# Two heads in each 32 rows: the query and key products of a first attention, packed and spread over its steps

## The chip, the cores and the metric

The kernel runs on one core of a Trainium2 chip. A core has five engines that take their instructions in order, each from its own queue, and that wait for each other through semaphores: TensorE (PE in the profile, with its weight loads shown apart as PEld), VectorE (DVE), ScalarE (ACT), GpSimd (POOL) and SyncE (SP, which here only starts transfers). The metric is the device time of one execution in microseconds (us), lower is better. Before the change three runs took 1332.35, 1331.23 and 1332.3 us, a median of 1332.3.

## What is computed

Two layers, each a cross-attention and a feed-forward, on `x` of 8 images with 256 tokens of 256 numbers, and a context of 8 x 256 tokens of 192 numbers. All is float32. The change touches the first cross-attention only. It has 16 heads of 16 numbers:

```python
q = (x @ Wq).reshape(B, N, 16, 16).transpose(0, 2, 1, 3)        # x is normed first
k = (context @ Wk).reshape(B, M, 16, 16).transpose(0, 2, 1, 3)
v = (context @ Wv).reshape(B, M, 16, 16).transpose(0, 2, 1, 3)
scores = jnp.einsum('bhid,bhjd->bhij', q, k) * 16 ** -0.5
scores = jnp.where(context_mask[:, None, None, :], scores, max_neg)
attn = jax.nn.softmax(scores, axis=-1)
out = jnp.einsum('bhij,bhjd->bhid', attn, v).transpose(0, 2, 1, 3).reshape(B, N, 256) @ Wo
```

After it come a mixture of 8 experts over all tokens, a second cross-attention with 16 heads of 64 numbers, and a channel mix. They are the larger part of the time and stay as they are.

## The kernel before

Tokens and heads. An image `b` has 256 tokens; a pair `p` of images (2p, 2p+1) shares one key tile `KT` of 128 partitions x 4 x 512. The 16 heads stand in four tiles `t` = 0..3 of four heads, each head in its own 32 partitions: rows 0 to 15 hold the 16 numbers of a head, row 16 the mask (for keys) or a one (for queries), row 17 of the keys a one, and row 17 of the queries the negated maximum of the scores. The host pads the weights with zeros to 32 columns for a head, so that a projection writes such a tile of 128 rows in one product. `QT` (128 x 4 x 256) holds an image's queries in the same layout, and has three buffers; `KT` has two.

The functions, by name:
- `keys0(p, t2)` makes two of the four key tiles of a pair: two products of 128 x 512 over the first 128 context numbers, and, from the closure `halves` that runs one step later, two products over the last 64 numbers, the one on the upper and the other on the lower 64 partitions. VectorE then adds `krows` (mask row and ones row) while it copies each tile out of PSUM.
- `queries0(b, t2)` makes two of the four query tiles: four products of 128 x 256, and one ScalarE activation of 128 x 512 that scales and puts the one into row 16 with a bias `cq` (loaded from the host).
- `key_rows(p)` computes `krows` for the pair's tokens from the mask: a reduction and three small VectorE operations, and two operations of 128 x 256 (VectorE for the first pair, GpSimd after that).
- `tokens0(b)` turns an image's normed tokens (made by `normed0`, on GpSimd from image 2 on) with four transposes; `values0(b)` makes the values; `project(b, qb)` is the output projection.
- `scores(q, k)`, `pair_maxima` and `values` are the attention itself. A step `h` makes the scores of one half tile twice: for query rows (`q`), whose maximum VectorE takes into `NM`, and, six steps later, for key rows (`k`), of which ScalarE takes the exponential into `ex`. Both write the same two buffers of PSUM (the tag `big`, two buffers); the two readers take turns on each buffer, and the next step's scores wait for both.

The order. `for h in range(8 * B + 12)` issues the steps. Within a step stand: the scores, the turning back of an output, the second halves of `keys0` and `values0` of the step before, `pair_maxima` (every fourth step), then what the table `whole` lists for this step (entered by `at(h, f)`), and `values` (every fourth step). TensorE, VectorE and GpSimd keep this order, so the `at` calls decide what stands in front of what. Eight steps are one image. In the steady part, an image's `queries0` stand 3 and 1 steps ahead of it, in whole halves of the head tiles, and a pair's `keys0` in steps 4 and 12 of 16. From step 47 on the first group's expert routing is mixed into the steps too.

The profile's line numbers: L103 is a helper through which VectorE and GpSimd operations of these steps go, L74 the matmul helper, L77 the transpose helper, L520 the query activation, L585 the exponential, L502 the copy of turned tokens.

Of the kernel before, what the change touches and what calls it, by code (L numbers as in the profile page):

```python
# [15 lines left out]
P = 128  # L16
# [6 lines left out]
BIG = float(2.0**100)  # L23
EPS = 1e-5


# [37 lines left out]
def kernel(ctx: ExitStack, tc: tile.TileContext, a: dict, out: bass.AP):  # L64
# [219 lines left out]
    with ExitStack() as l0:  # L284
# [3 lines left out]
        def load_ctx(p):  # L288
            cols = slice(512 * p, 512 * (p + 1))
            nc.sync.dma_start(ctx0T[:, cols], a["ctxT"][0:P, cols])  # L290
            if p == 0:
                load_mask(nc.sync, slice(0, 512))

            for h in range(2):
                nc.sync.dma_start(ctx1T[64 * h : 64 * h + 64, cols], a["ctxT"][P:C, cols])
            if p == 0:
                nc.sync.dma_start(cq, a["cq"])

# [4 lines left out]
        maskb = w0.tile([P, B * S], U8, name="maskb")  # L303
        cq = w0.tile([P, 1], F32, name="cq")

# [53 lines left out]

        krows = w0.tile([P, B * S], F32, name="krows")  # L360
        kscale = stat.tile([P, B], F32, tag="kscale", bufs=1, name="kscale")
        kshift = stat.tile([P, B], F32, tag="kshift", bufs=1, name="kshift")
        qscale = stat.tile([P, B], F32, tag="qscale", bufs=1, name="qscale")
        ones = stat.tile([P, 1], F32, tag="kones", bufs=1, name="kones")
        nc.vector.tensor_reduce(ones, ident[:, HD0 + 1 : P : 32], AX.X, ALU.add)

        def key_rows(p):
            two, tok = slice(2 * p, 2 * p + 2), slice(512 * p, 512 * (p + 1))

            tc.keep_in_program_order(  # L370
                vec.tensor_reduce(
                    anyk[:, two], maskb[:, tok].rearrange("p (b k) -> p b k", b=2), AX.X, ALU.max
                )
            )
            vec.tensor_scalar(kscale[:, two], anyk[:, two], cq, BIG, ALU.mult, ALU.mult)
            vec.tensor_scalar(kshift[:, two], kscale[:, two], -1.0, ones, ALU.mult, ALU.add)
            vec.tensor_scalar(qscale[:, two], anyk[:, two], HD0**-0.5, None, ALU.mult)
            for b in (2 * p, 2 * p + 1):
                (gps if p else vec).tensor_scalar(
                    krows[:, S * b : S * (b + 1)],  # L380
                    maskb[:, S * b : S * (b + 1)],
                    kscale[:, b : b + 1],
                    kshift[:, b : b + 1],
                    ALU.mult,
                    ALU.add,
                )

        ssq = stat.tile([P, E], F32, tag="ssq", bufs=1, name="ssq")
# [41 lines left out]

        NMs = [w0.tile([P, 2, 4, P], F32, name=f"NM0_{i}") for i in range(2)]
        for m in NMs:
# [3 lines left out]

        def keys0(p, t2):

            if t2 == 0:
                KT = p0.tile([P, 4, 512], F32, tag="KT", bufs=2, name=f"KT0_{p}")  # L440
                tos[2 * p]["KT"] = tos[2 * p + 1]["KT"] = KT
            KT = tos[2 * p]["KT"]
            tok = slice(512 * p, 512 * (p + 1))
            pk = [ps_mm(f"k0_{p}_{t2}_{h}") for h in range(2)]
            cols = [slice((2 * t2 + h) * P, (2 * t2 + h + 1) * P) for h in range(2)]
            for h in range(2):
                matmul(
                    pk[h], lhsT=wk[:, 0, cols[h]], rhs=ctx0T[:, tok], start=True, stop=False
                )

            def halves():
                for h in range(2):
                    r = slice(64 * h, 64 * h + 64)
                    matmul(
                        pk[h], lhsT=wk[r, 1, cols[h]], rhs=ctx1T[r, tok], start=False, stop=True
                    )
                for h in range(2):
                    tc.keep_in_program_order(
                        vec.tensor_tensor(
                            KT[:, 2 * t2 + h, :], pk[h], krows[:, tok], ALU.add  # L460
                        )
                    )

            return halves
# [38 lines left out]

        def queries0(b, t2):
            if t2 == 0:
                tos[b]["QT"] = p0.tile([P, 4, S], F32, tag="QT", bufs=3, name=f"QT0_{b}")
            pq = ps_mm(f"q0_{b}_{t2}").rearrange("p (t n) -> p t n", t=2)
            for i in range(2):
                t = 2 * t2 + i
                for c in range(2):  # L510
                    matmul(
                        pq[:, i, :],
                        lhsT=wq[:, c, t * P : (t + 1) * P],
                        rhs=tos[b]["xT"][:, c, :],
                        start=(c == 0),
                        stop=(c == 1),
                    )

            ways = 1 if (b, t2) == (0, 0) else 2
            nc.scalar.activation(  # L520
                tos[b]["QT"][:, 2 * t2 : 2 * t2 + ways, :],
                pq[:, 0:ways, :],
                AF.Identity,
                bias=cq,
                scale=qscale[:, b : b + 1],
            )
            if ways == 1:
                vec.tensor_scalar(
                    tos[b]["QT"][:, 1, :],
                    pq[:, 1, :],  # L530
                    qscale[:, b : b + 1],
                    cq,
                    ALU.mult,
                    ALU.add,
                )

        def scores(q, k):
# [8 lines left out]
            if k:  # L546
                b, t, kc = k
                for j in range(4):
                    r = slice(32 * j, 32 * j + HD0 + 2)
                    matmul(  # L550
                        sc[j // 2][:, j % 2, 1, :],
                        lhsT=tos[b]["KT"][r, t, b % 2 * S + kc * P : b % 2 * S + (kc + 1) * P],
                        rhs=tos[b]["QT"][r, t, :],
                        start=True,
                        stop=True,
                    )
            if q:
                b, t, qb = q
                for j in range(4):
                    r = slice(32 * j, 32 * j + HD0 + 1)  # L560
                    matmul(
# [10 lines left out]
            for i in range(2):  # L572
                if q:
                    vec.tensor_reduce(
                        NMs[(2 * b + t // 2) % 2][
                            :, qb, t, HD0 + 1 + 64 * i : 64 * i + 64 : 32
                        ],
# [12 lines left out]
        def pair_maxima(b, t2, to):  # L590
# [3 lines left out]
            for i in range(2):  # L594
                for qb in range(2):
                    transpose(pt[:, i, qb * P : (qb + 1) * P], nm[:, qb, 2 * t2 + i, :])
            qt = to["QT"][:, 2 * t2 : 2 * t2 + 2, :]
# [68 lines left out]

        tos += [{} for b in range(B)]
        stats0 = [ln_tiles(0, 2, "l0_0")]
        second = keys0(0, 0)
        tokens0(0)  # L670
        key_rows(0)
        second()
        queries0(0, 0)
        stats0 += [ln_tiles(2, 2, "l0_1")]
# [5 lines left out]
        for b, h in ((2, 4), (3, 6), (4, 15), (5, 23), (6, 31), (7, 39)):  # L680
            at(h, lambda b=b: normed0(b))
        at(0, lambda: keys0(0, 1))
        at(1, lambda: queries0(0, 1))
        at(1, lambda: tokens0(1))
        at(2, lambda: values0(0))
        at(3, lambda: queries0(1, 0))
        at(3, lambda: key_rows(1))
        at(4, lambda: keys0(1, 0))
        at(5, lambda: queries0(1, 1))
        at(6, lambda: tokens0(2))  # L690
        at(6, lambda: values0(1))
        at(7, lambda: queries0(2, 0))
        at(8, lambda: tokens0(3))
        at(9, lambda: queries0(2, 1))
        at(11, lambda: keys0(1, 1))
        for p in range(1, 4):
            h, b = 16 * (p - 1), 2 * p
            if h:
                at(h, lambda b=b: tokens0(b))
                at(h + 3, lambda p=p: key_rows(p))  # L700
                at(h + 4, lambda p=p: keys0(p, 0))
                at(h + 5, lambda b=b: queries0(b, 0))
                at(h + 7, lambda b=b: queries0(b, 1))
                at(h + 8, lambda b=b: tokens0(b + 1))
                at(h + 12, lambda p=p: keys0(p, 1))
            at(h + 13, lambda b=b: queries0(b + 1, 0))
            at(h + 15, lambda b=b: queries0(b + 1, 1))
            at(h + 17, lambda b=b: values0(b))
            at(h + 25, lambda b=b: values0(b + 1))

# [12 lines left out]
        for b in range(B):  # L723
            for qb in range(2):
                at(8 * b + 19, lambda b=b, qb=qb: project(b, qb, tos[b]))

# [3 lines left out]
        lgs = [[v.rearrange("p e d -> p (e d)") for v in u] for u in lgs]  # L730
        ems = [krows[:, 0:1024], krows[:, 1024:2048], wk.rearrange("p c f -> p (c f)")]
        dt = wq
# [973 lines left out]
```

## Time and profile before

| | us |
|---|---|
| median of three runs | 1332.3 |
| the profiled execution, its span | 1332.8 |
| first score product of the first attention (step 0) | 11.69 |
| step 9 begins | 41.48 |
| step 24 begins | 87.73 |
| step 40 begins (16 steps: 50.50) | 138.23 |
| step 47 begins | 160.92 |
| TensorE busy, whole span | 1315.3 (99%) |
| VectorE busy, whole span | 567.7 (43%) |
| ScalarE busy, whole span | 576.6 (43%) |
| GpSimd busy, whole span | 245.1 (18%) |

A row of the profile's list of groups gives the line, the engine, the operation, what it writes and reads, the shapes, the count, the busy time and the mean of one in ns, and then the idle time of the engine ahead of these instructions with what ended it. A line of the timeline gives start, length, engine, line, operation and count; the bracket at its end is the idle time of the engine ahead of it. TensorE runs a float32 product as two instructions, so that a 128 x 256 product counts twice. A line of the table of stretches gives the stretch and its length, then for PE, PEld, DVE, ACT and POOL the busy time with the number of instructions, the granted clock of TensorE (1.00 is full), the DMA share and GB/s.

### The profile page before, as it was taken

The page shows a single profiled execution, that of the slowest core. Times are in us where ns is not written, and L with a number is a line of the kernel's source. Part 1 is how long each engine was busy: PE and PEld are TensorE (multiplying, and loading weights), DVE is VectorE, ACT ScalarE, POOL GpSimd, SP SyncE. Part 2 cuts the span into 40 slices and gives each one's busy share as a digit, 9 for nine tenths or more (in the row PEclk, how much of TensorE's full clock was granted, in tenths as well). Part 3 has the DMA queues.
Part 4 walks back from the last instruction along what each step waited for, and adds up shares of the span by engine and source line. Part 5 has one row for each costly group of instructions (what it writes and reads, how often), then busy time and mean ns, then how long its engine had stood idle before and what let it go on. Part 6 is the DMA issues. An engine that isn't in the chain of part 4 may idle for free.

```text
span 1332.8 us, 19111 instructions
## 1 busy us (share of the span) xinstructions
PE 1315.3 (99%) x7520; PEld 955.6 (72%) x7520; DVE 567.7 (43%) x1131; ACT 576.6 (43%) x1396; POOL 245.1 (18%) x285
## 2 busy tenths in 40 slices
PE   9999999999999999999999999999999999999998
PEld 5666655577778786788867888866676676677777
DVE  6677777433320233322333110024544544544675
ACT  2644455353522363423634122213545445445653
POOL 3222412200000010100101000012323323333423
PEclk9999999899999999999999999999999999999999
DMA  7100000134134232342323434350000000000001
GB/s 218 65 1 2 1 1 1 63 103 134 68 134 134 70 132 78 124 134 72 130 82 120 134 118 151 103 154 1 0 1 1 1 1 1 1 1 1 1 8 56
DMA packets 59145, 86.85 MB, mean 65 GB/s; under 512 B 3376, under 2 KB 49072, under 8 KB 59056
## 3 DMA queue, kind: packets, MB, share of 16 engines
q1 hardware_dynamic: 58480, 85.11, 19.5%
q8 instruction: 59, 0.97, 0.3%
q10 hardware_dynamic: 576, 0.52, 0.1%
q14 instruction: 30, 0.25, 0.1%
HBM read 83.53 MB, written 2.10 MB: 64 GB/s over the span
## 4 chain that ended last, share of the span: by engine, by line
PE 94%; ACT 4%; DVE 2%; issue 0%; POOL 0%; ACTq 0%; DVEq 0%; POOLq 0%
PE ph L1104 17%; PE pe L1120 16%; PE sc L74 9%; PE q L74 7%; PE o L74 7%; PE po L74 5%; PE k L74 5%; PE pe L77 4%; PE v L74 4%; PE pc L1146 4%; PE pf L1050 3%; PE ln L968 3%; PE pf L74 1%; PE pk L74 1%; PE pr L74 1%; PE ln L74 1%
## 5 line engine op out<-in xcount | busy, mean ns | idle before, releaser
L1112 ACT ACTIVATE ht<-ph,b 128x256 f32<-128x256 f32 x256 | 119.3, 474 | 371.6 <-PE ph L1104 371.2
L1104 PE MATMUL ph<-slots,w 128*128 128x256 f32 x1024 | 266.9, 384 | 0.9 <-ACT ht L1112 0.2
L1120 PE MATMUL pe<-w,ht 128*128 128x256 f32 x1024 | 263.3, 381 | 0.0
L1104 PEld LDWEIGHTS ph<-slots,w 128*128 128x128 f32 x1024 | 182.3, 189 | 54.0 <-ACT ht L1112 21.7
L1120 PEld LDWEIGHTS pe<-w,ht 128*128 128x128 f32 x1024 | 192.0, 190 | 29.9 <-DVE slots L1129 4.2
L1379 POOL TENSOR_TENSOR ex<-ex,rz 128x1024 f32<-128x1024 f32 x64 | 119.9, 1895 | 229.9 <-DVE rz L1377 222.4
L1366 ACT ACTIVATE ex<-sc,nm 128x256 f32<-128x256 f32 x256 | 117.4, 484 | 53.0 <-DVE nm L1361 53.0
L585 ACT ACTIVATE ex<-sc 128x512 f32<-128x512 f32 x128 | 75.1, 598 | 68.7 <-PE sc L74 64.9
L74 PE MATMUL sc<-KT,QT 17*128 17x256 f32 (+1 forms) x1024 | 103.5, 380 | 0.8 <-ACT QT L520 0.7
L1028 POOL TENSOR_TENSOR es<-es,zs 128x1024 f32<-128x1024 f32 x12 | 22.7, 1894 | 432.8 <-DVE zs L1027 432.8
L103 DVE TENSOR_REDUCE NM<-sc 128x2 f32<-128x512 f32 x128 | 87.6, 691 | 32.7 <-PE sc L74 27.6
L1129 DVE TENSOR_TENSOR slots<-pe,b 128x512 f32<-128x512 f32 x32 | 22.1, 692 | 185.1 <-PE pe L1120 185.1
L74 PE MATMUL q<-xT,wq 128*128 128x256 f32 x384 | 94.9, 391 | 0.9 <-DVE xT L1276 0.9
L74 PEld LDWEIGHTS sc<-KT,QT 17*128 17x128 f32 (+1 forms) x1024 | 75.9, 186 | 20.8 <-issue 11.6
L74 PEld LDWEIGHTS q<-xT,wq 128*128 128x128 f32 x384 | 69.2, 189 | 28.1 <-issue 14.4
L1361 DVE TENSOR_REDUCE nm<-sc 128x4 f32<-128x1024 f32 x64 | 75.4, 1219 | 7.7 <-PE sc L74 4.7
L74 PE MATMUL po<-wo,ot 128*128 128x256 f32 x320 | 72.5, 382 | 0.0
L77 PE MATMUL pe<-ident,ex 128*128 128x128 f32 x512 | 70.2, 278 | 0.8 <-DVE et L1395 0.7
L74 PEld LDWEIGHTS po<-wo,ot 128*128 128x128 f32 x320 | 60.1, 190 | 10.9 <-issue 3.2
L77 PEld LDWEIGHTS pe<-ident,ex 128*128 128x128 f32 x512 | 56.5, 140 | 15.3 <-issue 7.6
L1395 ACT COPY et<-pe 128x512 f32<-128x512 f32 x64 | 37.5, 599 | 63.9 <-PE pe L77 63.4
L74 PE MATMUL o<-et,V 128*64 128x256 f32 x512 | 62.8, 385 | 0.8 <-ACT ot L1414 0.8
(227 smaller groups left out, 1665.9 us busy)
## 6 DMA issues: line engine op xcount, KB each, us to landing
w<-in_w_dram SPq DMA_DIRECT2D x64, 1024.0 KB, 5.7
b<-in_b_dram SPq DMA_DIRECT2D x32, 128.0 KB, 6.8
x_sb<-in_x_dram SPq DMA_DIRECT2D x3, 512.0 KB, 7.0
ctx0T<-in_ctxT_dram SPq DMA_DIRECT2D x4, 256.0 KB, 8.6
ctx1T<-in_ctxT_dram SPq DMA_DIRECT2D x8, 128.0 KB, 8.0
se<-in_slots_dram SPq DMA_DIRECT2D x1, 1024.0 KB, 11.1
wq<-in_wq_dram SPq DMA_DIRECT2D x1, 1024.0 KB, 5.1
wo<-in_wo_dram SPq DMA_DIRECT2D x1, 1024.0 KB, 12.1
```

The source lines that it names most:

```text
L74: tc.keep_in_program_order(nc.tensor.matmul(out, lhsT=lhsT, rhs=rhs, start=start, stop=stop))
L77: tc.keep_in_program_order(nc.tensor.transpose(out, in_, ident))
L103: ins = op(*args, **kwargs)
L585: nc.scalar.activation(ex[:, 2 - 2 * i : 4 - 2 * i, :], sc[1 - i][:, :, 1, :], AF.Exp)
L968: nc.tensor.matmul(pl[:, m * 512 : (m + 1) * 512], lhsT=st["xnT"][:, c, t * P : (t + 1) * P], rhs=snT[:, c, m * 512 : (m + 1) * 512], star ...
L1104: nc.tensor.matmul(ph, lhsT=c_["w1"][:, c, hc * P : (hc + 1) * P], rhs=slots[e][:, c * 256 : (c + 1) * 256], start=(c == 0), stop=(c == 1),)
L1112: nc.scalar.activation(ht, ph, AF.Gelu, bias=b1[:, e, hc : hc + 1])
L1120: nc.tensor.matmul(c_["pe"][:, b, :], lhsT=c_["ht"][hc][:, b * SL : (b + 1) * SL], rhs=c_["w2"][:, hc, :], start=(hc == 0), stop=(hc == HI ...
L1146: nc.tensor.matmul(pc[:, :D], lhsT=CT[:, bl, e, t * P : (t + 1) * P], rhs=eos[e][:, bl, :], start=(e == 0), stop=(e == E - 1),)
L1361: nc.vector.tensor_reduce(nm, sc, AX.X, ALU.max, negate=True)
L1366: nc.scalar.activation(ex[:, i, qb, :], sc[:, i, qb, :], AF.Exp, bias=nm[:, i, qb : qb + 1], accum_out=z[:, i, qb : qb + 1],)
L1379: nc.gpsimd.tensor_tensor(ex, ex, rz.rearrange("p h q -> p (h q)").unsqueeze(2).to_broadcast([P, 4, S]), ALU.mult,)
```

## The change

Each 32 rows now hold two heads in the projections' products: rows 0 to 15 one, rows 16 to 31 the other. `pack` makes the packed weights `wkd` and `wqd` on the core, with GpSimd copies out of the padded weights. A product then gives two of the four tiles at once (`u` = 0, 1 in place of `t` = 0..3), and two copies out of PSUM make the tiles `2u` and `2u + 1` from it: each multiplies by a factor for each row (`held`) that is 1 for its own 16 rows and 0 for the other 16. The mask and maximum rows of the odd tiles stand below their head (rows 15 and 14), and their score products read all 32 rows. `key_rows` makes two sets of `krows`, one for each of the two kinds of tile.

The order changes with it: a pair's keys are made in one place (step 7 of 16, the second half in step 8), with one of the two products in the PSUM buffer of the attention's output (`ps_o`); the queries of images 1 and 2 in one piece, of later images in two (4 and 5 steps into the eight for even images, 5 and 7 for odd ones); `tokens0(2)` moves from step 6 to step 5; the second half of the output projection of images 1, 3 and 5 moves one step later. The load of `cq` is gone, and `NM` is half as large.

```diff
-            vec.tensor_scalar(kscale[:, two], anyk[:, two], cq, BIG, ALU.mult, ALU.mult)
-            vec.tensor_scalar(kshift[:, two], kscale[:, two], -1.0, ones, ALU.mult, ALU.add)
-            vec.tensor_scalar(qscale[:, two], anyk[:, two], HD0**-0.5, None, ALU.mult)
-            for b in (2 * p, 2 * p + 1):
-                (gps if p else vec).tensor_scalar(
...
+            for v in range(2):
+                vec.tensor_scalar(
+                    kscale[:, v, two], anyk[:, two], masked[v], BIG, ALU.mult, ALU.mult
+                )
+                vec.tensor_scalar(
+                    kshift[:, v, two], kscale[:, v, two], -1.0, ones[v], ALU.mult, ALU.add
+                )
+                vec.tensor_scalar(
+                    qscale[:, v, two], anyk[:, two], held[v], HD0**-0.5, ALU.mult, ALU.mult
+                )
+                for b in (2 * p, 2 * p + 1):
+                    (gps if p or v else vec).tensor_scalar(
+                        krows[:, p % 2, v, S * (b % 2) : S * (b % 2 + 1)],
...
+        def pack(to, w, u):
+
+            for c in range(2):
+                gps.tensor_copy(
+                    to[:, u, c, :].rearrange("p (j s e) -> p j s e", j=4, s=2),
+                    w[:, c, :].rearrange("p (u s j e) -> p u j s e", u=2, s=2, j=4)[
+                        :, u, :, :, 0:HD0
+                    ],
+                )
+
+        def keys0(p, us):
...
+            pk = [(ps_o if u and len(us) > 1 else ps_mm)(f"k0_{p}_{u}") for u in us]
+            for i, u in enumerate(us):
                 matmul(
-                    pk[h], lhsT=wk[:, 0, cols[h]], rhs=ctx0T[:, tok], start=True, stop=False
+                    pk[i], lhsT=wkd[:, u, 0, :], rhs=ctx0T[:, tok], start=True, stop=False
                 )
...
+                for i, u in enumerate(us):
+                    for v in range(2):
+                        tc.keep_in_program_order(
+                            vec.scalar_tensor_tensor(
+                                KT[:, 2 * u + v, :],
+                                pk[i],
+                                held[v],
+                                krows[:, p % 2, v, :],
+                                ALU.mult,
+                                ALU.add,
+                            )
                         )
...
+            for v in range(2):
+                qt = tos[b]["QT"][:, 2 * us[0] + v : 2 * us[-1] + v + 1 : 2, :]
+                if v and b == 0 and us[0] == 0:
+                    vec.tensor_scalar(
+                        qt, pq, qscale[:, v, b : b + 1], masked[v], ALU.mult, ALU.add
+                    )
+                else:
+                    nc.scalar.activation(
+                        qt, pq, AF.Identity, bias=masked[v], scale=qscale[:, v, b : b + 1]
+                    )
...
+        pack(wkd, wk, 0)
+        pack(wqd, wq, 0)
         stats0 = [ln_tiles(0, 2, "l0_0")]
-        second = keys0(0, 0)
+        second = keys0(0, (0,))
...
-        at(0, lambda: keys0(0, 1))
-        at(1, lambda: queries0(0, 1))
+        at(0, lambda: pack(wkd, wk, 1))
+        at(0, lambda: pack(wqd, wq, 1))
+        at(0, lambda: keys0(0, (1,)))
+        at(1, lambda: queries0(0, (1,)))
...
-        at(3, lambda: queries0(1, 0))
+        at(3, lambda: queries0(1, (0, 1)))
         at(3, lambda: key_rows(1))
-        at(4, lambda: keys0(1, 0))
-        at(5, lambda: queries0(1, 1))
-        at(6, lambda: tokens0(2))
+        at(5, lambda: tokens0(2))
         at(6, lambda: values0(1))
-        at(7, lambda: queries0(2, 0))
+        at(7, lambda: keys0(1, (0, 1)))
         at(8, lambda: tokens0(3))
-        at(9, lambda: queries0(2, 1))
-        at(11, lambda: keys0(1, 1))
...
+        at(9, lambda: queries0(2, (0, 1)))
+        for b in range(3, B):
+            h = 8 * (b - 2)
+            if b > 3:
                 at(h, lambda b=b: tokens0(b))
...
+            if b % 2:
+                at(h + 5, lambda b=b: queries0(b, (0,)))
+                at(h + 7, lambda b=b: queries0(b, (1,)))
+            else:
+                at(h + 4, lambda b=b: queries0(b, (0,)))
+                at(h + 5, lambda b=b: queries0(b, (1,)))
+                at(h + 3, lambda b=b: key_rows(b // 2))
+                at(h + 7, lambda b=b: keys0(b // 2, (0, 1)))
```

## Prediction

> **What bounds the stage.** The page's busy times come first: TensorE 1315.3 of 1332.8 us, so work taken off it should shorten the span. Then I cut the first attention into steps, at each step's first score product in the timeline. Steps 32 and 33:
>
> ```profile
> 112.99 0.71 PE L74 MATMUL sc<-QT,KT 18*128 18x256 f32 x8
> ...
> 114.06 0.66 PE L77 MATMUL nm<-ident,NM 128*128 128x128 f32 x4
> 114.17 1.45 DVE L103 TENSOR_REDUCE NM<-sc 128x2 f32<-128x512 f32 x2 [0.69 <-PE sc L74]
> ...
> 114.29 1.21 ACT L585 ACTIVATE ex<-sc 128x512 f32<-128x512 f32 x2 [0.41 <-PE sc L74]
> ...
> 114.56 0.60 PE L77 MATMUL pt_x<-ident,xh_l 128*128 128x128 f32 x4
> ...
> 115.55 0.82 PE L74 MATMUL sc<-QT,KT 18*128 18x256 f32 x8 [0.39 <-ACT ex L585]
> ```
>
> A step's scores take 1.07 us (112.99 to 114.06). The next scores need the two buffers back, that is the two exponentials and two maxima: 2.56 us (115.55 - 112.99). That is a floor: TensorE had 2.1 us of work and waited 0.39. Steps 32 to 39 last 2.56, 2.68, 3.61, 3.01, 3.38, 4.06, 2.94 and 3.00: only work above 2.56 lengthens a step. VectorE is close behind, as step 20 shows:
>
> ```profile
> 73.87 0.71 PE L74 MATMUL sc<-QT,KT 18*128 18x256 f32 x8
> ...
> 74.29 0.65 DVE L103 TENSOR_REDUCE anyk<-maskb 128x2 f32<-128x512 uint8 x1
> ...
> 75.77 0.68 DVE L103 TENSOR_TENSOR x_sb<-po,x_sb 128x512 f32<-128x512 f32 x1
> 76.37 1.27 DVE L103 TENSOR_REDUCE NM<-sc 128x2 f32<-128x512 f32 x2
> ...
> 77.73 0.31 PEld L74 LDWEIGHTS sc<-QT,KT 18*128 18x128 f32 x8 [0.93 <-ACT ex L585]
> ```
>
> The scores were ready near 75.05, but VectorE still had the key rows and the projection's addition; the maxima came at 76.37, and the step took 3.86 where TensorE's work was about 3.4. The groups of steps 24 to 39, and one of the expert stage:
>
> ```profile
> L103 DVE TENSOR_REDUCE NM<-sc 128x2 f32<-128x512 f32 x32 | 22.1, 693 | 8.2 <-PE sc L74 7.1
> L585 ACT ACTIVATE ex<-sc 128x512 f32<-128x512 f32 x32 | 19.0, 598 | 21.8 <-PE sc L74 21.2 <-DVE NM L103 0.5
> ...
> L103 DVE TENSOR_TENSOR KT<-k,krows 128x512 f32<-128x512 f32 x4 | 2.6, 681 | 0.0
> ...
> L103 POOL TENSOR_SCALAR krows<-maskb,kscale,kshift 128x256 f32<-128x256 uint8 x2 | 1.1, 565 | 2.3 <-DVE qscale L103 2.3
> ...
> L1154 DVE SCALAR_TENSOR_TENSOR x_sb<-pc,rzn,x_sb 128x256 f32<-128x256 f32 x16 | 7.7, 484 | 77.0 <-PE pc L1146 77.0
> ```
>
> **What is taken away.** Four query products take 1.92 us (105.12 to 107.04 in the timeline). Each image needed eight and needs four: 8 x 1.92 = 15.4. Two key products take 1.81 and their second halves 1.06, where the two run beside each other; pairs 1 to 3 lose one such set each (8.6), pair 0 goes from 5.74 to about four single products of 0.91 (2.1). In all 26.1 us of TensorE work.
>
> **What of it the floor leaves.** With the new places, a step lasts the larger of its TensorE work and 2.58 (the floor and a little). Steps 16 to 23: 2.58, 2.58, 3.57 (values), 3.00 (projection), 2.58, 2.58, 2.94, 2.90 (keys), together 22.7; steps 24 to 31: 3.14 (key halves, maxima, turned tokens), 2.58, 3.57, 2.58, 2.58, 2.58, 2.94, 2.58, together 22.6. The 16 steps 24 to 39 give 45.3 against 50.5. Over steps 9 to 46 the same count gives 107.2 against 119.4 (160.92 - 41.48): -12.2. Step 47 goes from 3.44 to 2.58: -0.9. Together -13.1.
>
> **What comes back on VectorE, ScalarE and GpSimd.** The copies do not halve: each of a pair's four key tiles still takes one, and all four now come in one step with a third input. The trace has no such form at 128 x 512 out of PSUM. Bounds: 0.64, the spacing of two of today's additions (1.28 for two), and 0.97, twice the 128 x 256 row above. I take 0.72, near the lower end, as L1154 is only a seventh above an addition of its size (0.42). In step 24 (and 8, 40) VectorE then has the maxima until 2.6, four copies until 5.5 and the addition to QT until 6.1; the maxima of step 25 end their first half at 6.75, an exponential follows, and step 26 can begin at 7.45 where the count above had 3.14 + 2.58 = 5.7: +1.7, three times, 5.1. At 0.64 it is 1.4 each, at 0.97 it is 2.7.
>
> Key rows: three more small VectorE operations, about 0.6 us, in steps 19 and 35, where the cover of 3.4 to 3.9 us in steps 20 and 36 shrinks to 2.5 of TensorE work. By the chain of step 20 shown above that costs 1.9 and 1.2: 3.1. Query copies: `QT` of image 4 takes the buffer of image 1, whose last scores are in step 21. The copies of step 20 must wait for those, and the exponentials of step 21 stand behind them on ScalarE, and step 22's scores behind these: two copies of 0.56 (the one 128 x 256 row of L520), some 1.0 in steps 21 and 37: 2.0. Step 10, with two query copies of 0.78 ahead of its exponentials: 0.4. Sum 10.6; net -2.5.
>
> **The first nine steps.** GpSimd packs two 128 x 128 blocks before the first keys and two before the first queries. Bounds for a block: 0.20 (its 128 x 4 operations) and 0.61 (half of a 128 x 256 at 1.22); I take 0.4. The weights land first anyway, at about 8.3 for the queries, so these products start near 9.15 instead of 9.04; but only two of four stand ahead of the first scores, and the key rows no longer wait for `cq` (VectorE waited 1.1 us for it). The start gains about 0.7, of which the packing could take half. Then GpSimd is late:
>
> ```profile
> 29.79 4.84 POOL L103 TENSOR_SCALAR xh_l<-x_sb,mvp_l,rstdp_l 128x256 f32<-128x256 f32 x4
> ...
> 32.81 0.66 PE L77 MATMUL pt_x<-ident,xh_l 128*128 128x128 f32 x4
> ```
>
> Image 2's normed tokens were done at 32.24 and turned at 32.81, in step 6. Now two more `krows` operations (1.13) stand in front of them, TensorE has lost 4.9 us of keys and queries in steps 4 and 5, and the transposes are moved up to step 5. TensorE gets there near 28.0, the tokens are ready near 32.7: it waits 4.7 us, with all later scores behind it. Step 9 then starts near 43.1 against 41.48: +1.6, start included. So far: -13.1 + 10.6 + 1.6 = -0.9.
>
> **The clock.** Work turned into waits has a price that the sum lacks:
>
> ```profile
> 63.84:67.25 3.41, 2.72 (x25) 1.70 (x23) 2.83 (x6) 2.40 (x5) 0.00 (x0) 1.00 0.02 5
> 237.92:241.33 3.41, 1.82 (x13) 1.11 (x12) 1.94 (x6) 3.41 (x9) 0.00 (x0) 1.00 0.00 0
> 241.33:244.75 3.42, 2.75 (x13) 2.35 (x13) 1.38 (x2) 1.09 (x3) 0.00 (x0) 0.50 0.00 0
> 244.75:248.16 3.41, 3.41 (x28) 1.75 (x32) 0.69 (x1) 1.63 (x8) 0.00 (x0) 0.50 0.01 2
> ```
>
> These are stretches of half the 6.83 us for which the granted clock stood at 0.50 (241.33 to 248.16). It fell after a stretch with TensorE busy for 1.82 of 3.41 us, and held in one with 2.72. In the new order, TensorE waits 4.7 us in step 5, and 1.5 to 2.2 in steps 9, 11, 20, 21, 25, 37 and 41. Step 5 surely halves the clock; the products of steps 6 and 7 at half rate cost about 1.6. Of the seven others, some 2.5 should hit a stretch that holds most of the wait (it depends on where the stretches lie). A drop costs between 0 (the next steps wait anyway) and 3.4 (all of 6.83 us at half rate); a step with 2.04 us of work grows from 2.58 to 4.08, which over 6.83 us is 2.5; I take 2.2. So 1.6 + 2.5 x 2.2 = 7.1.
>
> The Trainium skill ("TensorE: Matmul & The Clock Gate", section "HAM oscillation") has the clock fall after idle gaps of more than some 3.4 us. By that rule only step 5 would trip it, and the sum would be 1333.0. The row above, where a wait of 1.46 us was enough, speaks against it.
>
> **Sum.** -0.9 + 7.1 = +6.2. The profiled execution (1332.8) lies 0.5 above the median, so: 1332.8 + 6.2 - 0.5 = 1338.5.
>
> **The rivals.**
> - The clock holds. For: 2.46 of 3.41 us near 910 did not trip it, and most of the new steps keep TensorE busy for 2.04 of 2.58. Against: the drop at 241.33. Then 1332.3 - 0.9 = 1331.4, or 1333.0 with step 5 alone: no change.
> - The gain stays. Place: the maxima of the steps after the key copies and key rows. If VectorE's chain is shorter than I count, the 10.6 is not given back, and -13.1 + 1.6 gives 1320.8: faster. It decides once four copies and an addition end within about 4.4 us of their step's start (6.1 by my count). Against it stands step 20, which was late already.
> - The clock stays low. If a busy share near 0.6 to 0.75 already trips it, about eight drops of 2.5 us follow: 1332.3 - 0.9 + 20 = 1351.
> - The change does not do what it says: excluded as far as the instruction order shows, since the products are halved there.
>
> **How the numbers follow.** Forecast 0.55, clock holds 0.25, gain stays 0.10, clock stays low 0.10. A measurement here can tell about 0.2%, 2.7 us, from nothing. Faster: the gain that stays (0.10) and the fast edge of the clock that holds (0.04): 0.14. Same: 0.17 of the clock that holds and 0.02 of the forecast: 0.19. Slower: 0.67. The range runs from 1330 (the lower edge of the clock that holds) to 1347 (four or five more drops, or copies of 0.97); it leaves out the gain that stays and most of the clock that stays low. The forecast's own range is 1334 to 1345.
>
> **What would show it.** Right: steps 11 to 13, 27 to 29 and 45 near 2.6; a 4 to 5 us wait of TensorE for GpSimd's `xh_l` near 28; steps 20, 25, 36 and 41 above 3.7 with late maxima; stretches at clock 0.50 between 30 and 160 us. Wrong: full clock all through the attention, key copies at another price, or steps 20 and 25 near 2.6. If the span from the first scores to the experts changes by much less than the total, the cause is elsewhere.

## The result, and the profile after

The changed kernel is slower: 1342.9 us (four runs, 1342.57 to 1344.32) against 1332.3, a ratio of 1.0084 (95% interval 1.0072 to 1.0096), so 10.6 us. The page of the changed kernel, its busy times, TensorE and its granted clock over 40 slices of 33.5 us:

```profile
span 1340.7 us, 18958 instructions
## 1 busy us (share of the span) xinstructions
PE 1306.4 (97%) x7424; PEld 945.6 (71%) x7424; DVE 571.2 (43%) x1148; ACT 578.0 (43%) x1407; POOL 250.3 (19%) x301
...
PE   7899999999999999999999999999999999999998
...
PEclk8789999999999999999999999999999999999999
```

Work did go: 8.9 us less of TensorE's busy time. But the first three digits of the clock fell, and the busy time holds what ran at half rate. Starts of steps, from the timelines:

| starts at (us) | before | changed | changed - before |
|---|---|---|---|
| step 0 | 11.69 | 11.09 | -0.60 |
| step 9 | 41.48 | 48.34 | +6.86 |
| step 24 | 87.73 | 100.45 | +12.72 |
| step 40 | 138.23 | 149.29 | +11.06 |
| step 48 | 164.36 | 173.43 | +9.07 |
| step 69 | 236.55 | 246.19 | +9.64 |
| end of the span | 1332.8 | 1340.7 | +7.9 |

The time is lost before step 24 (12.72 us); from there to step 48 the change gains 3.65 us back, as it was meant to. The table of stretches of the changed kernel (TensorE's busy time is the first pair behind the length, the clock the third number from the end):

```profile
11.68:15.10 3.42, 2.21 (x14) 0.90 (x10) 2.79 (x9) 0.30 (x1) 0.32 (x2) 1.00 0.85 269
15.10:18.51 3.41, 3.41 (x9) 1.39 (x6) 2.06 (x4) 0.00 (x0) 0.00 (x0) 0.50 1.04 332
28.75:32.16 3.41, 1.77 (x12) 0.83 (x11) 3.34 (x11) 0.72 (x2) 2.67 (x12) 1.00 0.48 93
32.16:35.58 3.42, 0.47 (x1) 0.18 (x1) 1.10 (x3) 0.00 (x0) 3.42 (x5) 0.50 1.03 396
49.23:52.64 3.41, 2.18 (x16) 1.44 (x8) 3.38 (x8) 1.38 (x5) 0.00 (x0) 1.00 0.00 0
56.06:59.47 3.41, 2.00 (x33) 1.26 (x26) 2.90 (x9) 1.59 (x4) 0.86 (x3) 1.00 0.00 0
59.47:62.88 3.41, 3.06 (x21) 1.97 (x20) 1.97 (x3) 1.59 (x4) 2.16 (x11) 0.50 0.00 0
86.78:90.19 3.41, 1.29 (x18) 0.72 (x16) 2.86 (x7) 0.84 (x2) 2.91 (x10) 1.00 0.00 0
90.19:93.60 3.41, 3.41 (x20) 2.38 (x20) 1.90 (x4) 2.77 (x6) 1.29 (x7) 0.50 0.00 0
```

Four times the clock halves behind a stretch in which TensorE was busy for 1.29 to 2.21 of 3.41 us: at 15.10, 32.16 and 59.47 for 10.24 us, at 90.19 for 6.83. Other stretches as thin passed, such as that of 2.18 at 49.23. The forecast wait of step 5, in the timeline:

```profile
27.92 0.71 PE L77 MATMUL sc<-KT,QT 17*128 17x256 f32 x8
...
31.27 2.18 POOL L106 TENSOR_SCALAR krows<-maskb,kscale,kshift 128x256 f32<-128x256 uint8 x4
...
33.43 4.83 POOL L106 TENSOR_SCALAR xh_l<-x_sb,mvp_l,rstdp_l 128x256 f32<-128x256 f32 x4
34.71 0.47 PE L80 MATMUL pt_x<-ident,xh_l 128*128 128x128 f32 x1 [3.00 <-POOL xh_l L106]
35.91 0.90 PE L80 MATMUL pt_x<-ident,xh_l 128*128 128x128 f32 x3 [0.73 <-POOL xh_l L106]
```

Four key-row operations of GpSimd stand ahead of the normed tokens, and TensorE waits 3.73 us (3.00 + 0.73) for the tokens. The clock fell at 32.16, when the first of these waits (from 31.71 on) had lasted 0.45 us; the stretch ahead of it, with 1.77 us of work, holds a wait of 1.18 us for the maxima of step 4 as well (up to 30.41). Step 20 has the late maxima:

```profile
84.44 0.71 PE L77 MATMUL sc<-QT,KT 32*128 32x256 f32 x8
...
84.86 0.65 DVE L106 TENSOR_REDUCE anyk<-maskb 128x2 f32<-128x512 uint8 x1
...
87.20 0.68 DVE L106 TENSOR_TENSOR x_sb<-po,x_sb 128x512 f32<-128x512 f32 x1
87.80 1.28 DVE L106 TENSOR_REDUCE NM<-sc 128x2 f32<-128x512 f32 x2
...
89.16 0.71 PE L77 MATMUL sc<-QT,KT 32*128 32x256 f32 x8 [2.12 <-ACT ex L614]
```

The addition comes 2.34 us after the reduction of the mask began (87.20 - 84.86; before 1.48, 75.77 - 74.29), since eight small operations lie between (before five): six of the key rows (before three) and two of the expert slots. The step lasts 4.72 us against 3.86. And in step 24 the four key copies:

```profile
102.99 2.72 DVE L106 SCALAR_TENSOR_TENSOR KT<-k,krow,krows 128x512 f32<-128x512 f32 x4
...
105.63 0.68 DVE L106 TENSOR_TENSOR QT<-nm,QT 128x512 f32<-128x512 f32 x1
106.22 1.28 DVE L106 TENSOR_REDUCE NM<-sc 128x2 f32<-128x512 f32 x2
...
107.59 0.71 PE L77 MATMUL sc<-QT,KT 18*128 18x256 f32 x8 [0.51 <-ACT ex L614]
```

Step 25 begins at 103.61 and ends at 107.59: 3.98 us, where the forecast without the copies was 2.58. The table of stretches for just this step has TensorE busy for 2.84 us of it and VectorE for all of it:

```profile
103.61:107.59 3.98, 2.84 (x25) 1.82 (x24) 3.98 (x8) 1.78 (x3) 0.00 (x0) 1.00 0.00 0
```

### The profile page after: what moved, and what is told of

It reads as the page before. It is cut to its first block, busy times and chain, and to the rows that moved or that the text cites. A ratio compares the mean times of both kernels' runs of the same rounds, so it can differ in the third digit from the quotient of the medians.

```text
span 1340.7 us, 18958 instructions
## 1 busy us (share of the span) xinstructions
PE 1306.4 (97%) x7424; PEld 945.6 (71%) x7424; DVE 571.2 (43%) x1148; ACT 578.0 (43%) x1407; POOL 250.3 (19%) x301
## 4 chain that ended last, share of the span: by engine, by line
PE 90%; ACT 4%; DVE 4%; issue 1%; POOL 1%; DMA 0%; ACTq 0%; DVEq 0%; POOLq 0%
PE ph L1134 17%; PE pe L1150 16%; PE sc L77 9%; PE o L77 7%; PE q L77 5%; PE po L77 5%; PE pe L80 4%; PE v L77 4%; PE pc L1176 4%; PE k L77 4%; PE pf L1080 3%; PE ln L998 3%; ACT ex L614 1%; PE pf L77 1%; PE pk L77 1%; PE pr L77 1%
## 5 line engine op out<-in xcount | busy, mean ns | idle before, releaser
L77 PE MATMUL sc<-KT,QT 64*128 64x256 f32 (+2 forms) x1024 | 107.6, 394 | 3.0 <-DVE NM L106 2.4
L77 PEld LDWEIGHTS sc<-KT,QT 64*128 64x128 f32 (+2 forms) x1024 | 78.4, 194 | 23.6 <-issue 11.8
L77 PE MATMUL q<-xT,wq 128*128 128x256 f32 x256 | 63.0, 391 | 0.9 <-DVE xT L1306 0.9
L77 PE MATMUL sc<-QT,KT 32*128 32x256 f32 (+1 forms) x512 | 49.8, 448 | 10.5 <-ACT ex L614 10.5
```

The source lines that it names most:

```text
L77: tc.keep_in_program_order(nc.tensor.matmul(out, lhsT=lhsT, rhs=rhs, start=start, stop=stop))
```

## The experiments

**The clock by itself.** If the low clock is what the change pays, TensorE must be kept busy without anything else being moved. The fill is transposes of the identity into a spare PSUM buffer, at the end of five steps, and in the same way ahead of the token transposes of step 5:

```diff
+        fills = {0: 6, 9: 7, 11: 8, 20: 12, 36: 6}
...
+            if h in fills:
+                to = ps_o(f"fill_{h}")
+                for i in range(fills[h]):
+                    transpose(to[:, 0:P], ident)
```

> The changed kernel with idle TensorE time filled: transposes of the identity into a spare PSUM buffer at the end of steps 0 (6), 9 (7), 11 (8), 20 (12) and 36 (6), and 18 ahead of the token transposes of step 5, in waits of 1.2 to 3.7 us. Nothing else moves. Theory (the halved clock costs most of the 10.6 us, and a stretch of 3.41 us with TensorE busy for less than some 2.2 us halves it): no stretch at clock 0.50 between 8 and 110 us, the time falls to 1335.5 (1333 to 1338). Rival (the products at half rate fall into steps that wait for VectorE or GpSimd anyway): the clock stays up but the time stays above 1340. Rival (the clock does not follow the busy share): the stretches at 0.50 stay, time 1343 to 1346.

Measured: 1332.59 us, ratio to the kernel before 1.0002 (0.9992 to 1.0011). Pure waste, 57 transposes, makes the changed kernel 10.3 us faster. The fill of step 5 in its timeline, then one stretch at the place of the drop of 59.47 (step 12) and the one with the wait of step 20, behind which the drop of 90.19 had come:

```profile
29.15 2.19 PE L80 MATMUL fill_tokens<-ident 128*128 128x128 f32 x18
...
32.25 0.33 PE L80 MATMUL pt_x<-ident,xh_l 128*128 128x128 f32 x1 [0.91 <-POOL xh_l L106]
33.45 0.55 PE L80 MATMUL pt_x<-ident,xh_l 128*128 128x128 f32 x3 [0.88 <-POOL xh_l L106]
```

```profile
54.72:58.13 3.41, 2.63 (x37) 1.73 (x31) 2.43 (x7) 1.63 (x5) 2.00 (x10) 1.00 0.02 5
78.61:82.02 3.41, 2.60 (x24) 2.22 (x26) 3.34 (x9) 0.71 (x2) 3.08 (x9) 1.00 0.00 0
```

The wait of step 5 is still there (2.19 filled, 0.91 and 0.88 left: 4.0 us), so it is not the wait that was removed. Two short drops of 3.41 us stay (at 20.58 and 34.24), all others are gone. So the first theory holds in its cause, not in its sizes: it had excluded any drop here, and 1332.59 lies just below its range. What is left without low clock is no gain and no loss: step 9 starts at 44.48 (+3.0 against before), step 48 at 163.50 (-0.86). From the start of step 9 to that of step 48 it takes 119.02 us against 122.88, 3.9 less.

**GpSimd's order.** The one edit: `at(3, lambda: key_rows(1))` becomes `at(4, ...)`, which puts the rows behind `normed0(2)`.

> The changed kernel with the key rows of pair 1 made in step 4, behind image 2's normed tokens on GpSimd, in place of step 3, in front of them. Theory (TensorE's wait in step 5 is for GpSimd, whose four key-row operations of 2.18 us stand ahead of the tokens): image 2's tokens are ready 2.2 us after the roots earlier, the wait of step 5 shrinks by 2.2, step 9 starts near 46.2 in place of 48.34, the time is 1340.7; other stretches of low clock may move by one in either way (2.5 us each). Rival (step 5 is late for the clock and the statistics alone): step 9 within 0.5 of 48.3, time 1342 to 1344.

Measured: 1335.45 us, ratio 1.0026 (1.0014 to 1.0038). The forecast part is there: from GpSimd's first operation for these tokens to their first transpose it takes 4.70 us (25.95 to 30.65) against 6.70 (28.01 to 34.71). Step 9 starts at 46.41, close to the 46.2 of the theory, but that is partly luck: the first drop lasted 6.83 us in place of 10.24, the second 13.65 in place of 10.24, and the two nearly cancel. And the time gained 7.4 us and not 2.2: in this execution the third drop did not come (the stretches ahead of it had 2.21 and 2.00 busy) and the fourth lasted 3.41. Ten runs of this one kernel spread from 1331.91 (mean granted clock 0.993) to 1340.09 (0.987), so which drops come, and for how long, differs from execution to execution; a single such comparison can't price an edit here.

**Packing without the new order.** Products and copies as in the change, at the places that keys, queries, tokens and projections had before:

```diff
+        at(3, lambda: queries0(1, (0,)))
+        at(4, lambda: keys0(1, (0,)))
+        at(5, lambda: queries0(1, (1,)))
+        at(6, lambda: tokens0(2))
...
+            at(h + 4, lambda p=p: keys0(p, (0,)))
+            at(h + 12, lambda p=p: keys0(p, (1,)))
```

> The packed products of the changed kernel at the places that keys, queries, tokens and projections had before: two key copies or two query copies in a step, never four. Theory (the gain is given back because four key copies, doubled key rows and moved tokens meet in few steps): the steps of queries and keys end near 2.6 each, about 0.44 us less in each of some 20 query places and 0.5 to 0.9 in six key places, no wait of TensorE above 2 us in step 5 and at most one stretch of low clock: 1325 (1322 to 1329). Rival (the doubled copies and key rows themselves eat the gain, wherever they stand): 1331 or more. Rival (steps of 2.04 us of work in 2.58 are too thin for the clock): several stretches at 0.50 after 40 us, 1335 or more.

Measured: 1335.96 us, ratio 1.0028 (1.0016 to 1.004). The first theory fell with its number. The number and the drops of the last rival are what the trace shows, at 13, 78, 133 and 242 us; its reason, steps too thin for the clock, is not, as a single wait of 1.42, 2.13, 1.23 and 1.46 us stands at each:

```profile
9.91:13.32 3.41, 1.77 (x10) 0.61 (x10) 2.95 (x9) 0.54 (x2) 1.00 (x4) 1.00 0.82 254
...
74.76:78.17 3.41, 1.28 (x8) 0.45 (x10) 3.34 (x11) 0.95 (x2) 2.99 (x8) 1.00 0.00 0
...
129.37:132.79 3.42, 2.27 (x19) 1.16 (x20) 2.69 (x5) 1.56 (x3) 0.73 (x2) 1.00 0.00 0
...
238.60:242.01 3.41, 1.82 (x13) 1.11 (x12) 1.86 (x5) 3.41 (x9) 0.00 (x0) 1.00 0.00 0
```

Between the drops the steps are shorter, as expected (24 to 36: 35.20 us against 37.12 before). Step 20 lasts 4.72 here too, though keys stand in it and not queries: what it shares with the changed kernel is the doubled key rows.

**The two cures, alone and together.** At the old places again: (a) fill; (b) the six small key-row operations of pairs 2 and 3 on GpSimd; (c) both.

```diff
+            small = gps if p > 1 else vec
             for v in range(2):
-                vec.tensor_scalar(
+                small.tensor_scalar(
                     kscale[:, v, two], anyk[:, two], masked[v], BIG, ALU.mult, ALU.mult
```

> Packed products at the old places, with TensorE's waits filled by transposes of the identity at the end of steps 0 (6), 4 (6), 20 (12), 36 (6) and 69 (7). Theory (without low clock the old places keep about 1.1 us in steps 9 to 20, 1.9 in 24 to 36 and 2.3 in 40 to 48 against before, and lose 0.9 and 0.4 in steps 20 and 36; the stretches of low clock of the run without fill, at 13, 78, 133 and 242 us, cost the rest): no stretch at 0.50 after 20 us, 1326 (1324 to 1329). Rival (the fill only helped where the order had changed): 1333 or more. Rival (filling takes TensorE time that the steps need): steps 20 and 36 longer than 4.72 and 3.82, 1331 or more.

> Packed products at the old places, with the six small operations of the key rows of pairs 2 and 3 on GpSimd in place of VectorE, nothing filled. Theory (steps 20 and 36 last 4.72 and 3.82 because VectorE does 1.5 us of small operations ahead of the projection's addition and the maxima): step 20 falls to 3.2 and step 36 to 2.9 (some 2.4 us together), TensorE's wait there shrinks from 2.13 to under 0.7, the stretches of low clock at 78 and 133 us go: 1330 (1328 to 1332.5). Rival (the projection's addition or the slots' scale on VectorE sets these steps): step 20 above 4.0, time 1334 to 1337.

> Both: key rows' small operations of pairs 2 and 3 on GpSimd, and fill at the end of steps 0 (6), 4 (6), 20 (3), 36 (3) and 69 (7). Theory (late VectorE and low clock are what gives the gain back, and they add up): 1324 (1321 to 1327), the fastest of all, no low clock after 20 us. Rival (with the waits gone the steps of 2.58 themselves trip the clock): stretches at 0.50 in places without a long wait, 1329 or more.

Measured: (a) 1325.83 us, ratio 0.9943 (0.9931 to 0.9956); (b) 1327.15, 0.9958 (0.9946 to 0.9971); (c) 1321.58, 0.9917 (0.9904 to 0.9931). (a) is the forecast to 0.2 us, and its steps 20 and 36 keep their 4.71 and 3.81, so the fill takes nothing from them; one early drop stays in its profile (17.36 to 24.18). (b) is faster than its range, and shortens step 20 to 3.23 and step 36 to 2.56, 2.75 us together; its timeline has the addition at once behind the slots' operations, and the rows beside it:

```profile
79.78 0.26 POOL L106 TENSOR_SCALAR kscale<-anyk,krow 128x2 f32<-128x2 f32 x1 [2.30 <-DVE nt_slots L106]
...
79.89 0.68 DVE L106 TENSOR_TENSOR x_sb<-po,x_sb 128x512 f32<-128x512 f32 x1
...
80.49 1.27 DVE L106 TENSOR_REDUCE NM<-sc 128x2 f32<-128x512 f32 x2
...
81.84 0.71 PE L77 MATMUL sc<-QT,KT 32*128 32x256 f32 x8 [0.64 <-ACT ex L615]
```

With the wait of step 20 down from 2.13 to 0.64 us the drops at 78 and 133 are gone too, without fill. The one at 242 is gone as well, though this edit does not touch that place; in the kernel before, too, only some executions have it, as shown further down. Two early ones stay (at 12.19 and 32.67). (c) has the clock at 1.00 until its last microsecond, so steps of 2.58 us do not lower the clock by themselves. It is the fastest of all: 10.5 us faster than before, 21.3 faster than the change as it stands.

**What the new order costs with both cures.** The same cures on the changed kernel's own order, with the key rows of pair 1 one step later (`at(4, ...)`).

> The changed kernel with its own order, but the key rows of pair 1 in step 4, the six small key-row operations of pairs 2 and 3 on GpSimd, and the waits filled (steps 0, 9, 11, 20, 36, 69 with 6, 7, 8, 3, 3, 7 transposes, and 10 ahead of the tokens of step 5). Theory (beside late VectorE and low clock, the new order itself costs: TensorE waits for GpSimd's tokens in step 5, and four key copies delay the maxima in steps 8, 24 and 40): 1327.5 (1325.5 to 1330), some 6 us behind the same cures at the old places; steps 25 and 41 stay near 3.97. Rival (the order is harmless once the clock holds and VectorE is freed): within 2 us of 1321.6.

Measured: 1329.2 us, ratio 0.9972 (0.9962 to 0.9982). The order is not harmless, but the 7.6 us between the medians are not all its own, since the fill does not hold the clock here. The profiled execution starts step 48 at 159.21, that of (c) at 153.36. Of the 5.85 us, 2.95 lie ahead of step 9, where the wait for GpSimd is still 0.73 + 0.88 us behind 1.31 of fill, and where two drops of 3.41 us stay (at 18.61 and 32.26). The other 2.90 come at full clock: 1.06 in steps 9 to 18, 1.34 in steps 24 to 27, where step 25 with its four key copies still takes 3.97 against 2.74, and 0.50 elsewhere. The one run with a mean clock of 0.999 took 1326.09, 4.5 above (c); this is the nearest that the record has to the price of the order alone.

**The drop of the kernel before.** The same fill there, seven transposes at the end of step 69.

> The kernel before with seven transposes of the identity at the end of step 69, in its 1.46 us wait at 239.73. Theory (a wait of 1.46 us, with TensorE busy for 1.82 of 3.41 us, halves the clock for 6.83 us, which costs some 1.8 us): no stretch at 0.50 near 241, 1330.5. Rival (the stretch at half rate lies beside waits for ScalarE): within 0.5 of 1332.2. Rival (the clock falls there for another reason): the stretch stays.

Measured: 1331.98 us, ratio 0.9996 (0.9987 to 1.0005). The drop is gone from the profile:

```profile
237.18:240.59 3.41, 2.93 (x23) 2.22 (x21) 1.96 (x6) 3.41 (x10) 0.00 (x0) 1.00 0.00 0
240.59:244.01 3.42, 2.39 (x24) 1.90 (x28) 1.64 (x5) 2.29 (x8) 0.00 (x0) 1.00 0.01 2
```

and from step 69 to the end the span is 2.85 us shorter (1093.4 against 1096.25). But the median is what it was: the number is the rival's, though a drop was there and had its price. The runs explain it: in each of these experiments a profiled execution's own time lies 1.75 to 2.2 us above its span (here 1331.45 and 1329.7; for (c) 1321.01 and 1318.8). So the profiled execution of before, with a span of 1332.8, took about 1334.8, and belongs to the few: of the 49 times of before in the three sets of comparisons 9 lie at 1334.1 to 1334.9, the others at 1331.1 to 1332.8. The mean granted clock that is recorded with each of them agrees: 0.997 in all nine, which is what one drop of 6.83 us at half clock makes of a span of 1332.8 (1 - 0.5 x 6.83 / 1332.8), and 0.998 to 1.0 in the other 40. In the filled kernel it is 1.0 in all eleven.

**A last wait.** (c) with image 1's token transposes in step 2 in place of step 1.

> The fastest version so far (old places, small key-row operations on GpSimd, fill) with image 1's token transposes in step 2 behind the values' first half, in place of step 1, where TensorE waits 1.29 us for VectorE's normed tokens. Theory (that wait is on the path): steps 1 and 2 together 0.8 to 1.3 us shorter, 1320.6. Rival (the next scores wait for the maxima anyway): within 0.5 of 1321.6.

Measured: 1322.11 us, ratio 0.9926 (0.991 to 0.9943), not different from (c), whose runs lie between 1320.84 and 1322.61. The wait of 1.29 us came back in step 2 as 1.68 us for the same tokens, part of it behind a drop of 3.41 us at 16.25 that (c) does not have. So the rival holds in its outcome (0.5 us from 1321.6), though not in its reason.

## Why the prediction was right, and where its sizes were off

The forecast, slower by about 6 us because the gain is given back on VectorE and the thinner work lets the clock fall, held; 1342.9 lies in the range. The range reached down to no change at all, so that alone says little; the runs say more. Filling alone takes 10.3 of the 10.6 us away, so the low clock is shown as what makes the changed kernel slower, and (b) shows that late VectorE work is part of what gives the gain back. Term by term:

- **Work taken away: 26.1, too large** (the sum does not use it). In (c), which has the same products and the clock at 1.00, TensorE without the fill is busy for 1294.3 us (1297.8 - 3.5), in the kernel before without its drop for 1311.9 (1312.8 - 0.9): 17.6.
- **Steps 9 to 47, -13.1 + 10.6 = -2.5:** 3.9 less in the filled kernel. Both halves were a little large: what came back adds up to 7.9 (taken 10.6), so some 11.8 were gained (taken 13.1). Key copies went by 0.68 us each (2.72 for four; taken 0.72) and cost 1.4 in step 9 (4.44 against 3.05 before) and 1.4 each in steps 25 and 41 (3.97 against the 2.58 of the forecast), together 4.1 (taken 5.1). Key rows: 2.75, from steps 20 and 36 with and without the small operations on VectorE (taken 3.1). The copies into `QT` that wait for the next scores: steps 21 and 22 take 2.89 and 3.17 in the cured new order against 2.58 and 2.94, 0.5 in each image (taken 1.0); this wait is read off the traces only and not shown by an experiment: a fourth buffer of `QT`, which would have taken it away, doesn't fit into memory, so that run gave no time. Step 10: nothing (taken 0.4).
- **The first nine steps, +1.6 without the clock:** +3.0. Four key-row operations and the moved tokens were rightly named (a wait of 3.73 from 31.71 on, 4.0 in the filled kernel; 4.7 from near 28 on forecast). Step 6 starts there at 33.93 against 31.73, step 8 now holds the second halves of the keys (3.16 against 2.56), and two short drops are still in these 3.0. This term and the one before were off by 1.4 each, in opposite ways: that step 48 starts 0.86 earlier in the filled kernel, as the forecast's -0.9 has it, is luck.
- **The clock, 7.1: the term that was most mis-sized; 10.3 measured.** The step that failed is "Step 5 surely halves the clock; the products of steps 6 and 7 at half rate cost about 1.6": up to step 9 the low clock cost 3.9 (48.34 - 44.48). A drop at 15.10 had come before it, out of one wait of 1.21 us for the first step's maxima, and was not in the forecast; it made step 3's maxima late, and with them GpSimd's start (28.01 against 25.41 before). And drops lasted up to 10.24 us where 6.83 had been taken. The later part came out near the forecast: 5.5 for 2.5 drops of 2.2, 6.05 measured between steps 9 and 24 (52.11 - 46.06), but for two drops of some 3.0, so fewer and dearer ones.
- **The base.** "The profiled execution (1332.8) lies 0.5 above the median" compared a span with times. By the 1.75 to 2.2 us found above it lay some 2.5 above it, for a drop that most runs do not have. So 7.9 between the spans became 10.6 between the medians.

Of the rivals, "the clock holds" (1331.4, or 1333.0 with step 5 alone) is what the filled kernel shows: 1332.6. "The gain stays" fell: VectorE's chain was late nearly as counted. "The clock stays low", with eight drops and 1351, fell too: there were four. The rule of the Trainium skill ("TensorE: Matmul & The Clock Gate", section "HAM oscillation"), a gap of more than some 3.4 us, is not what these traces show: three of the four drops followed waits of at most 1.21, 1.41 and 2.12 us, and the fourth came 0.45 us into the wait of step 5, behind one of 1.18.

## What to carry to other kernels

Before taking work off an engine that is 99% busy, ask stage by stage what will end last there; here a floor of 2.56 us per step and late copies turned much of it into waits, and of 17.6 us of TensorE work taken away the best order gained 10.5. A wait of TensorE that costs nothing by itself can cost through the clock, so look at the granted clock in stretches, not only at its mean, and try a few idle transposes as a diagnosis: they separate the cost of the wait from that of the clock. Spread copies and row operations over steps, and move the small ones to an engine that idles, before moving the products.

## What the runs showed of the hardware that was not expected

The clock's rule is not a simple share of busy time. Between 8 and 250 us, stretches at full clock with TensorE busy for 1.83 of 3.41 us or less were followed by half clock in ten cases of eleven; the eleventh (1.73, in the last experiment) came right behind a drop. Of those with 1.86 to 2.3 seven of 23 were: 2.00, 2.20 and 2.27 each fell in one run and held in another. And it fell three times after 2.72 to 2.87. Drops lasted 3.41, 6.83, 10.24 or 13.65 us, whole numbers of such stretches. In each execution all drops begin and end on one grid of 3.41 us, and the grid lies elsewhere in each. That fits the different times of one and the same kernel, but no run tests it, and what decides between the lengths stays open.
